# A planner's cost for ScalarE, and a state-space layer put in its written order

## The chip, the cores and the metric

The kernel runs on one core of a Trainium2 chip, in one launch. The metric is device time in microseconds; the time before is the median of three runs. Every execution timed here is of the whole network: eight layers, from the load of `x` to the store of the output.

## The reference

Four blocks of two layers each act on `x` of 8 sequences by 256 positions by 128 features. Every layer is wrapped as `x = x + layernorm(layer(layernorm(x)))`, where this layernorm has no weights. All data is float32. The layers are a gated delta rule, a local attention, a Plücker attention, a ternary feed-forward net, an attention, a mixture of experts, a two-way state-space layer (Mamba) and a quantized feed-forward net. The change touches the first six through one number of a planner, and the seventh, Mamba, in its code. What the seventh computes:

```python
def _mamba(x, W_in, conv_w, conv_b, W_xp, W_dt, dt_b, A_log, Dp, W_out):
    xp, z = split(x @ W_in.T)
    xc = silu(causal_conv4(xp) + conv_b)                 # E = 256 channels
    dt_lo, Bm, Cm = split(xc @ W_xp.T)                   # N = 64 states
    dt = softplus(dt_lo @ W_dt.T + dt_b)
    A = -exp(A_log)
    # for every position t:
    #   h = exp(dt * A) * h + (dt * xc)[:, :, None] * B[:, None, :]
    #   y = sum over n of h[:, :, n] * C[n]
    y = (y + xc * Dp) * silu(z)
    return y @ W_out.T

xn = layernorm(x) * ln1_w + ln1_b
x1 = _mamba(xn, m1)
x2 = flip(_mamba(flip(xn), m2))
out = layernorm(x1 + x2) * ln2_w + ln2_b + xn
```

As the wrapper normalizes `x` before the call, the layer's first layernorm is the second of two in a row on the same data. A second layernorm of a row with variance v has the variance v/(v+eps), so both together divide by sqrt(v*(1+eps) + eps*eps) if they are done as one.

## The kernel before

**The first six layers** are cut into small tasks (Python generators). A planner, the class `Turns`, runs them: it keeps a clock for each engine, adds the estimated time of each instruction that a task's step issues (`issued`), and always picks the live step that could begin first. The time that it gives an instruction of ScalarE (ACT) is `190 + 0.83 n` ns for n elements per partition, whatever the source, and 1283 ns more when the table of functions changes. The order that comes out is nailed down by `as_written`, which ties each instruction of the tensor engine (PE), VectorE (DVE), ACT and GpSimd (POOL) to the one before it on the same engine. The estimate decides more than the order: `Turns.evac` gives a copy out of PSUM to ACT or to DVE, whichever clock is behind, and `Turns.ps` fills gaps of PE with spare matmuls.

**Layer seven, `l3_attn`**, is not tied: its program order is a wish, and the framework's scheduler may issue ready instructions of an engine in another order. Its work is 8 units: four groups of two sequences (512 columns), each with two directions (m = 0 and 1). A unit's recurrence is done one state at a time, 64 states, so the loop has 8 x 64 = 512 steps `i`. In step `i` the program writes:

- `pre`: POOL makes the tile `dB` (one for two odd states, L2040);
- `inputs` of state i-1: PE writes `ps_h` in PSUM, by transposes of `sT` (even states, L2068) or by 64x64 matmuls (odd states, L2066);
- `start` of state i: a DMA brings `Cs`; ACT makes `sT` (even states, four instructions, L2050) and `dA` (two exponentials, L2053);
- `scan` of state i-1: DVE's scan (L2074) makes `h` from `dA` and `ps_h`; POOL multiplies it by `Cs` into `hc` (L2076); in every eighth state DVE does this product too;
- `add` of state i-4: PE adds `hc` to `ps_y` by transposes (L2086).

A unit also has a `prologue` (norm for m = 0, convolution, projections, SiLU, softplus: everything up to `dt`, `dtxT`, `B`, `cd`), and an `epilogue` (copy of `ps_y`, product with silu(z), output projection, and for m = 1 the norms and the residual). Both are generators: each `yield` hands over to the next step of the loop, so a `yield` between a producer and its consumer is a distance of one state in program order. The prologue of unit u+1 starts at state 6 of unit u; the epilogue of unit u-1 starts in unit u when its last state has been added. `norm_steps` is used by all layers: statistics on DVE (L227, L228), the power -1/2 on POOL (L230, L231), four `yield`s, a product on DVE (L234), one `yield`, and four ACT instructions (L237).

The buffers that set distances: `h`, `dA`, `sT` and `dB` have three each, `Cs` five, `hc` four. PSUM has three slots of two banks for `ps_h` and for every intermediate product `ps_a` of prologue and epilogue together (the function `pb`), and one slot of two banks for `ps_y`.

Of the kernel before, what the change touches and what calls it, by code (L numbers as in the profile page):

```python
# [17 lines left out]
P = 128  # L18
NB = 8
L = 256  # L20
# [152 lines left out]
class Ctx:  # L173
# [46 lines left out]
    def norm_steps(self, dst, src, n):  # L220

        nc = self.nc
        st = self.small.tile([P, n, 6], F32, name="ln_st")
        mv = self.small.tile([P, n, 2], F32, name="ln_mv")
        rs = self.small.tile([P, n], F32, name="ln_rs")
        for i in range(n):
            nc.vector.bn_stats(out=st[:, i, :], in_=src[:, i, :])  # L227
            nc.vector.bn_aggr(out=mv[:, i, :], in_=st[:, i, :])  # L228
        yield
        nc.gpsimd.tensor_scalar(rs, mv[:, :, 1], EPS, None, ALU.add)  # L230
        nc.gpsimd.tensor_tensor(rs, rs, self.mhalf.to_broadcast([P, n]), ALU.pow)  # L231
        for i in range(4):
            yield
        nc.vector.scalar_tensor_tensor(mv[:, :, 0], mv[:, :, 0], -1.0, rs, ALU.mult, ALU.mult)  # L234
        yield
        for i in range(n):
            nc.scalar.activation(dst[:, i, :], src[:, i, :], AF.Identity, bias=mv[:, i, 0:1], scale=rs[:, i:i + 1])  # L237
        yield
# [46 lines left out]
class Turns:  # L285
# [105 lines left out]
    def issued(self, ins):  # L391
# [6 lines left out]
        if "PE" in e:  # L398
            self.matmul(ins, aps)
            return  # L400
        elif "Pool" in e:
            t = 350.0 + (1.6 if n > 64 else 160.0 if "pow" in str(getattr(ins, "op", "")) else 2.0) * n
        elif "Act" in e:
            t, f = 190.0 + 0.83 * n, str(getattr(ins, "func", ""))
            table = next((x for x in ("Silu", "Gelu", "Sqrt") if x in f), "Exp" if "Exp" in f or "Tanh" in f else self.tables)
            if table != self.tables:
                self.tables, t = table, t + 1283.0
        else:
            t = (165.0 if op != "TensorScalarPtr" else 205.0) + 1.03 * n
# [1438 lines left out]
def l3_attn(k):  # L1848
# [17 lines left out]
    with ExitStack() as es:  # L1866
# [10 lines left out]
        for m, w in enumerate(k.l3a):  # L1877
# [8 lines left out]
            nc.vector.tensor_scalar(w["A"], w["A"], 1e-20, -1.0, ALU.max, ALU.mult)  # L1886
        xTs, CLs = [], []
# [21 lines left out]
        def prologue(u, o):  # L1909
            g, m = divmod(u, 2)  # L1910
            w = k.l3a[m]
            if m == 0:
                xs = xns[g] = s2.tile([P, 4, D], F32, name="xn")
                yield from k.norm_steps(xs, k.x[:, 4 * g:4 * g + 4, :], 4)
                yield from k.norm_steps(xs, xs, 4)
                nc.gpsimd.tensor_tensor(xs, xs, over(k.l3a_ln[:, 0, :], 4, 1), ALU.mult)
                nc.gpsimd.tensor_tensor(xs, xs, over(k.l3a_ln[:, 1, :], 4, 1), ALU.add)
                yield
            xT, CL = xTs[u % 2], CLs[u % 2]
            ps = pb()  # L1920
            for j in range(4):
# [3 lines left out]
                else:  # L1925
                    nc.tensor.matmul(ps[:, 0, d], xns[g][:, j ^ 1, :], k.flip, start=True, stop=True)
            yield
# [5 lines left out]
            for ec in range(2):  # L1933
                for b in range(2):
# [3 lines left out]
                    yield  # L1938
                    nc.scalar.activation(xc[:, ec, b * L:(b + 1) * L], ps[:, 0, 0:L], AF.Identity, bias=w["cols"][:, ec, 0:1])
                    yield  # L1940
                    yield
            for ec in range(2):
                ps = pb()
                nc.tensor.matmul(ps[:, 0, :], w["win"][:, 256 + ec * P:256 + (ec + 1) * P], xT[:, :, 3:3 + L], start=True, stop=True)
                yield
# [11 lines left out]
            yield  # L1957
            B = s2.tile([P, 4, N], F32, name="B")
# [10 lines left out]
            yield  # L1969
            nc.scalar.activation(dt, ps, AF.Softplus)  # L1970
# [6 lines left out]
            yield  # L1977
            dtxT = s2.tile([P, 4, 2, P], F32, name="dtxT")
            ps = pb()
            for j in range(4):  # L1980
                for ec in range(2):
                    n = 2 * j + ec
                    nc.tensor.transpose(ps[:, n // 4, n % 4 * P:(n % 4 + 1) * P], dtx[:, ec, j * P:(j + 1) * P], k.ident)
            yield
# [3 lines left out]
        def epilogue(u, o):  # L1988
# [4 lines left out]
            yield  # L1993
            py = pb()
# [3 lines left out]
            yield  # L1998
            t = s2.tile([P, 2, U], F32, name="t", tag="sp_u")
            for ec in range(2):  # L2000
                nc.vector.scalar_tensor_tensor(t[:, ec, :], o["xc"][:, ec, :], w["cols"][:, ec, 2:3], py[:, ec, :], ALU.mult, ALU.add)
            yield
            nc.gpsimd.tensor_tensor(t, o["sz"], t, ALU.mult)
# [6 lines left out]
            xs = s2.tile([P, 4, D], F32, name=f"x1{m}")  # L2010
            yield
# [8 lines left out]
            yield  # L2020
            xs = x1s[g]
            nc.vector.tensor_tensor(xs, ps[:, 0, :].rearrange("p (i d) -> p i d", d=D), xs, ALU.add)
            yield from k.norm_steps(xs, xs, 4)
# [5 lines left out]
            yield  # L2029
            yn = s2.tile([P, 4, D], F32, name="yn")  # L2030
            yield from k.norm_steps(yn, xs, 4)
# [38 lines left out]
        def scan(st, n):  # L2070
# [4 lines left out]
            st["hc"] = s1.tile([P, 2, 2, L], F32, name="hc", bufs=4)  # L2075
            (nc.vector if on_v else nc.gpsimd).tensor_tensor(st["hc"], h, over(by_seq(st["C"]), 2, 2), ALU.mult)  # L2076

        def add(o, st, n):

            if n == 0:  # L2080
                o["py"] = psumy.tile([P, 4, 2, P], F32, name="ps_y")
            for b in range(2):
                for j in range(2):
                    for ec in range(2):
                        first = n == 0 and j == ec == 0
                        nc.tensor.matmul(  # L2086
                            o["py"][:, 2 * b + j, ec, :], st["hc"][:, b, ec, j * P:(j + 1) * P], k.ident,
                            start=first, stop=n == N - 1, is_transpose=True, skip_group_check=True,
# [10 lines left out]
        for i in range(units * N + 4):  # L2099
# [15 lines left out]
            if i >= 4:  # L2115
                v, c = divmod(i - 4, N)
                add(made[v], sts.pop(i - 4), c)
# [57 lines left out]
def program(tc, I, out, layers):  # L2175
    nc = tc.nc
    with ExitStack() as es:
# [39 lines left out]
        for layer in (l3_attn, l3_ffn):  # L2217
            if layer in layers:
                layer(k)
# [20 lines left out]
```

## Time and profile before

| what | us |
|---|---|
| median of three runs | 4112.87 |
| the three runs | 4107.72 to 4126.58 |
| the profiled execution, its own time | 4108.04 |
| its span, first to last instruction | 4106.3 |
| start of the first scan of layer seven | 2671.2 |
| end of DVE's last product of layer seven | 4022.96 |
| busy in the whole span: PE, DVE, ACT, POOL | 3556.8, 3015.5, 2541.2, 2651.4 |

Times within the execution are counted from the start of the span. Busy times are unions of an engine's instructions; a wait is idle time of an engine, put down to what ended it. A busy PE is not PE at its peak, since matmuls are pipelined: the distance from start to start tells its rate.

### The profile page before, as it was taken

To read this page: it belongs to the slowest core of one execution; us is meant where nothing else is said; L and a number is where in the kernel's file an instruction comes from. 1 tells how busy PE (TensorE), PEld (TensorE's weight loads), DVE (VectorE), ACT (ScalarE), POOL (GpSimd) and SP (SyncE) were. 2 spreads that over 40 slices of the span, in tenths; PEclk is the share of its full clock that TensorE was granted. 3 is DMA by queue.
4 is the path that set the end of the run, shared out by engine and by line. 5 is a ranking of instruction groups with operands and counts; after the bars stand their busy time and mean duration, and the time that the engine had idled before them with its cause. 6 is when DMAs were issued, how large, how long until landed. Compare 5 with 4: busy or idle time off the path is not lost. (4 is left out here: it accounts for less than half of the span.)

```text
span 4106.3 us, 125005 instructions
## 1 busy us (share of the span) xinstructions
PE 3556.8 (87%) x55183; PEld 2808.9 (68%) x55183; DVE 3015.5 (73%) x4210; ACT 2541.2 (62%) x4481; POOL 2651.4 (65%) x1991
## 2 busy tenths in 40 slices
PE   6899898988898888899998977698988988898886
PEld 4777787777777656565565554387777876877774
DVE  7667768767666666654477677289979988998995
ACT  4445455544445545565454443399979988898893
POOL 5666857856665554522133344389989988998993
PEclk8999999999999999999999998799999999999997
DMA  2000000000001000000000000033323333333430
GB/s 58 3 3 2 3 3 2 3 3 8 3 23 34 1 1 12 20 6 21 1 1 1 6 1 1 26 105 112 110 81 116 111 100 93 111 112 91 115 114 26
DMA packets 98677, 168.89 MB, mean 41 GB/s; under 512 B 16699, under 2 KB 26582, under 8 KB 98006
## 3 DMA queue, kind: packets, MB, share of 16 engines
q1 hardware_dynamic: 98134, 160.89, 13.2%
q8 instruction: 433, 7.09, 0.7%
q14 instruction: 110, 0.90, 0.1%
HBM read 153.51 MB, written 2.10 MB: 38 GB/s over the span
## 5 line engine op out<-in xcount | busy, mean ns | idle before, releaser
L2076 POOL TENSOR_TENSOR hc<-h,Cs 128x1024 f32<-128x1024 f32 x448 | 1050.1, 2373 | 97.8 <-DVE h L2074 85.8
L2074 DVE TENSOR_TENSOR_SCAN h<-dA,ps_h 128x1024 f32<-128x1024 f32 x448 | 989.1, 2267 | 88.9 <-PE ps_h L2068 54.0
L2053 ACT ACTIVATE dA<-dt,A 128x512 f32<-128x512 f32 x1024 | 684.4, 715 | 125.1 <-DVE h L2074 92.2
L2086 PE MATMUL ps_y<-w_c_ident,hc 128*128 128x128 f32 x4096 | 560.9, 281 | 116.1 <-POOL hc L2076 84.1
L2086 PEld LDWEIGHTS ps_y<-w_c_ident,hc 128*128 128x128 f32 x4096 | 453.0, 143 | 171.4 <-POOL hc L2076 156.0
L2050 ACT ACTIVATE sT<-dtxT,B 128x256 f32<-128x256 f32 x1024 | 449.8, 495 | 5.7 <-PE ps_h L2068 5.7
L590 DVE SCALAR_TENSOR_TENSOR acc<-ps,w_l0a_conv,acc 128x254 f32<-128x254 f32 (+2 forms) x768 | 310.3, 472 | 46.9 <-ACT acc L584 46.7
L2066 PE MATMUL ps_h<-dB,dtxTt 64*64 64x64 f32 x16384 | 301.8, 223 | 19.3 <-DVE h L2074 10.1
L2066 PEld LDWEIGHTS ps_h<-dB,dtxTt 64*64 64x64 f32 x16384 | 266.2, 136 | 72.9 <-issue 46.4
L2068 PE MATMUL ps_h<-w_c_ident,sT 128*128 128x128 f32 x2048 | 277.3, 280 | 19.5 <-DVE h L2074 16.9
L2068 PEld LDWEIGHTS ps_h<-w_c_ident,sT 128*128 128x128 f32 x2048 | 240.2, 145 | 31.6 <-DVE h L2074 23.9
L742 POOL TENSOR_TENSOR Ps<-M,w_c_levels 128x512 f32<-128x512 f32 x192 | 241.3, 1274 | 7.2 <-DVE M L716 6.2
L230 POOL TENSOR_SCALAR ln_rs<-ln_mv 128x4 f32<-128x4 f32 (+1 forms) x84 | 22.0, 263 | 336.8 <-DVE ln_mv L228 307.0
L359 ACT COPY XY<-ps 128x1024 f32<-128x1024 f32 (+1 forms) x116 | 108.6, 947 | 152.8 <-PE ps L807 140.5
L800 PE MATMUL ps<-Z,XY 64*64 64x64 f32 x4608 | 169.5, 224 | 21.8 <-DVE Z L784 14.5
L807 PE MATMUL ps<-XY,Z 64*64 64x64 f32 x5120 | 168.8, 222 | 3.5 <-issue 3.5
L800 PEld LDWEIGHTS ps<-Z,XY 64*64 64x64 f32 x4608 | 142.1, 135 | 42.2 <-DVE Z L784 19.3
L1633 ACT ACTIVATE e<-ps,nm 128x256 f32<-128x256 f32 x256 | 99.9, 481 | 96.8 <-DVE nm L1630 69.5
L781 PE MATMUL ps<-XY,Ps 64*64 64x64 f32 x5120 | 115.9, 226 | 48.4 <-issue 11.7
L2074 DVE TENSOR_TENSOR_SCAN ps_h<-dA,ps_h 128x1024 f32<-128x1024 f32 x64 | 145.6, 2275 | 14.9 <-PE ps_h L2066 14.6
L784 DVE TENSOR_TENSOR Z<-ps,w_c_ident 128x512 f32<-128x512 f32 x160 | 107.8, 686 | 60.1 <-PE ps L781 58.6
L807 PEld LDWEIGHTS ps<-XY,Z 64*64 64x64 f32 x5120 | 148.6, 136 | 4.2 <-issue 4.2
(452 smaller groups left out, 8559.8 us busy)
## 6 DMA issues: line engine op xcount, KB each, us to landing
Cs<-cd SPq DMA_DIRECT2D x512, 256.0 KB, 3.3
dtxTt<-dtxT SPq DMA_DIRECT2D x32, 128.0 KB, 4.0
wk<-in_l0a_w SPq DMA_DIRECT2D x8, 256.0 KB, 6.8
w_h<-in_l1f_h SPq DMA_DIRECT2D x4, 512.0 KB, 6.0
w_l2a<-in_l2a_w SPq DMA_DIRECT2D x3, 512.0 KB, 3.8
w_l0a_wg<-in_l0a_wg SPq DMA_DIRECT2D x1, 1024.0 KB
w_qk<-in_l0f_wqkv SPq DMA_DIRECT2D x2, 512.0 KB, 5.3
cv<-in_l3a_m_conv SPq DMA_DIRECT2D x2, 512.0 KB, 4.9
```

Source lines behind the costliest of these rows:

```text
L590: nc.vector.scalar_tensor_tensor(acc[:, n, s:L], p4[:, n, 0:L - s], conv[:, h2, 4 * j + n, 3 - s:4 - s], acc[:, n, s:L], ALU.mult, ALU.add,)
L742: nc.gpsimd.tensor_tensor(t, M[:, :, 0:64], over(k.l0a_levels[:, n, :], 8, 1), ALU.mult)
L781: nc.tensor.matmul(ps[to, a, at(j)], Ps[own, h, :], XY[own, t, at(i)], start=True, stop=True)
L800: nc.tensor.matmul(ps[own, a, at(j)], XY[rows, t, at(i)], Z[rows, za, at(zj)], start=True, stop=True)
L807: nc.tensor.matmul(ps[to, a, at(4 + j)], Z[rows, za, at(zj)], XY[rows, t, at(i)], start=True, stop=True)
L2050: nc.scalar.mul(st["s"][:, j], o["dtxT"][:, j], o["B"][:, j, n:n + 1])
L2053: nc.scalar.activation(dA[:, :, ec, :], by_seq(o["dt"][:, ec, :]), AF.Exp, scale=w["A"][:, ec, n:n + 1])
L2066: nc.tensor.matmul(ps[q, b, ec, j * 64:(j + 1) * 64], o["dtxTt"][rows, j, ec, q], dB[rows, j, :], start=True, stop=True)
L2068: nc.tensor.transpose(ps[:, j // 2, ec, j % 2 * P:(j % 2 + 1) * P], st["s"][:, j, ec, :], k.ident)
L2074: nc.vector.tensor_tensor_scan(h.rearrange(flat), st["dA"].rearrange(flat), st["in"].rearrange(flat), 0.0, ALU.mult, ALU.add)
L2076: (nc.vector if on_v else nc.gpsimd).tensor_tensor(st["hc"], h, over(by_seq(st["C"]), 2, 2), ALU.mult)
L2086: nc.tensor.matmul(o["py"][:, 2 * b + j, ec, :], st["hc"][:, b, ec, j * P:(j + 1) * P], k.ident, start=first, stop=n == N - 1, is_transpos ...
```

## The change

1. The planner's estimate for an ACT instruction of the first six layers: `140 + 0.83 n` ns where an input lies in PSUM, `310 + 0.75 n` where all lie in SBUF.
2. `l3_attn` is put under `as_written` for PE, DVE, ACT and POOL.
3. `add` works on state i-5 in place of i-4; `hc` has five buffers.
4. More `yield`s in prologue and epilogue: two in place of one between most PE products and the copies that read them; in the norms three before and three after the product on DVE.
5. The two layernorms at the head of the layer are one, with the variance of both (`twice`).
6. `xc * D`: before, two DVE instructions with `D` as a scalar (L2001) in the epilogue. After, eight fp32 matmuls of `xc` by a diagonal tile `D` begin the sum in `ps_y`; DVE's single product takes `ps_a` and silu(z), and POOL's product `t` (L2003) goes.

```diff
-    def norm_steps(self, dst, src, n):
+    def norm_steps(self, dst, src, n, twice=False, steps=(4, 1)):
...
-        nc.gpsimd.tensor_scalar(rs, mv[:, :, 1], EPS, None, ALU.add)
+        if twice:
+            nc.gpsimd.tensor_scalar(rs, mv[:, :, 1], 1.0 + EPS, EPS * EPS, ALU.mult, ALU.add)
+        else:
+            nc.gpsimd.tensor_scalar(rs, mv[:, :, 1], EPS, None, ALU.add)
         nc.gpsimd.tensor_tensor(rs, rs, self.mhalf.to_broadcast([P, n]), ALU.pow)
-        for i in range(4):
+        for i in range(steps[0]):
             yield
         nc.vector.scalar_tensor_tensor(mv[:, :, 0], mv[:, :, 0], -1.0, rs, ALU.mult, ALU.mult)
-        yield
+        for i in range(steps[1]):
+            yield
...
-            t, f = 190.0 + 0.83 * n, str(getattr(ins, "func", ""))
+            near = any(a.bass_ap.space == PSUM for a in aps[len(ins.outs):])
+            t, f = 140.0 + 0.83 * n if near else 310.0 + 0.75 * n, str(getattr(ins, "func", ""))
...
+            w["D"] = s1.tile([P, 2, P], F32, name="D", bufs=2)
+            for ec in range(2):
+                nc.vector.tensor_scalar(w["D"][:, ec, :], k.ident, w["cols"][:, ec, 2:3], None, ALU.mult)
...
-                yield from k.norm_steps(xs, k.x[:, 4 * g:4 * g + 4, :], 4)
-                yield from k.norm_steps(xs, xs, 4)
+                yield from k.norm_steps(xs, k.x[:, 4 * g:4 * g + 4, :], 4, True, (3, 3))
...
             t = s2.tile([P, 2, U], F32, name="t", tag="sp_u")
-            for ec in range(2):
-                nc.vector.scalar_tensor_tensor(t[:, ec, :], o["xc"][:, ec, :], w["cols"][:, ec, 2:3], py[:, ec, :], ALU.mult, ALU.add)
-            yield
-            nc.gpsimd.tensor_tensor(t, o["sz"], t, ALU.mult)
+            nc.vector.tensor_tensor(t, py, o["sz"], ALU.mult)
+            yield
             yield
             yield
...
-            st["hc"] = s1.tile([P, 2, 2, L], F32, name="hc", bufs=4)
+            st["hc"] = s1.tile([P, 2, 2, L], F32, name="hc", bufs=5)
...
             if n == 0:
                 o["py"] = psumy.tile([P, 4, 2, P], F32, name="ps_y")
+                for j in range(4):
+                    for ec in range(2):
+                        nc.tensor.matmul(
+                            o["py"][:, j, ec, :], o["xc"][:, ec, j * P:(j + 1) * P], w["D"][:, ec, :],
+                            start=j % 2 == ec == 0, stop=False, skip_group_check=True,
+                        )
...
-            if i >= 4:
-                v, c = divmod(i - 4, N)
-                add(made[v], sts.pop(i - 4), c)
+            if i >= 5:
+                v, c = divmod(i - 5, N)
+                add(made[v], k.l3a[v % 2], sts.pop(i - 5), c)
...
-                layer(k)
+                with as_written(tc, COMPUTE if layer is l3_attn else ()):
+                    layer(k)
```

The further lines of the diff are single `yield`s: one more before the ACT copies of `xT`, the convolution, `sz`, `CL` and `B`, `dt`, `dtxT`, and `x1`, one more before the transposes of `yT` and one after them, one more before DVE's sum of `x1` and `x2`, two more before the transposes of `dtx`, three more before the transposes of `xn`, and one before the last norm.

## The prediction

> **What bounds the kernel now.** I read the page's head and slices first, then the busy times cut by the 8 units of layer seven, then who waited for whom on DVE in that loop, then the timeline of its worst stretch.
>
> ```profile
> span 4106.3 us, 125005 instructions
> PE 3556.8 (87%) x55183; PEld 2808.9 (68%) x55183; DVE 3015.5 (73%) x4210; ACT 2541.2 (62%) x4481; POOL 2651.4 (65%) x1991
> ```
>
> No engine is full over the span, but the shares mix two regimes. Up to about 2620 us the first six layers run, with PE busiest. The loop of layer seven, first scan 2671.2 to last product 4022.96, is 1351.8 us. I cut it where each unit's first scan starts (units 0, 1, 2, 6, 7; columns are the stretch, its length, then busy time of PE, PEld, DVE, ACT, POOL, the granted clock, the DMA share, GB/s):
>
> ```profile
> 2671.20:2832.60 161.40, 146.81 (x2888) 127.93 (x2891) 150.29 (x72) 151.37 (x283) 147.54 (x73) 0.97 0.36 108
> 2832.60:2995.90 163.30, 147.88 (x2924) 130.81 (x2920) 151.86 (x75) 149.08 (x275) 151.79 (x76) 0.99 0.37 110
> 2995.90:3182.00 186.10, 157.22 (x2936) 138.03 (x2934) 158.62 (x112) 156.03 (x291) 164.44 (x90) 0.94 0.32 97
> ...
> 3694.60:3870.10 175.50, 151.23 (x2940) 133.33 (x2936) 155.12 (x95) 152.33 (x283) 159.50 (x84) 0.98 0.37 103
> 3870.10:4022.90 152.80, 132.95 (x2833) 118.94 (x2821) 150.87 (x75) 129.29 (x241) 148.33 (x72) 0.99 0.36 109
> ```
>
> Unit 7, which prepares no other, takes 152.8 us with DVE busy 150.87: DVE is the floor (in the timeline eight states of a bare stretch take 18.7 us from scan to scan, 2.34 a state), and ACT and POOL stand within some per cent of it wherever a prologue runs. Unit 2 (unit 4 is its twin with 186.7) takes 33 us more than unit 7, of which only 8 are work of DVE. So the loop loses to DVE's idle time. DVE's waits within the loop:
>
> ```profile
> DVE h L2074 <- PE ps_h L2068: 54.0, 17, 35.7
> DVE ln_mv L234 <- POOL ln_rs L231: 30.4, 10, 3.7
> DVE h L2074 <- PE ps_h L2066: 15.9, 15, 3.2
> DVE ps_h L2074 <- PE ps_h L2066: 14.6, 6, 3.4
> DVE ln_st L227 <- POOL x L2028: 13.3, 3, 4.5
> DVE t L2001 <- PE ps_a L1997: 8.3, 7, 1.9
> DVE h L2074 <- POOL hc L2076: 8.2, 9, 1.8
> ```
>
> The 35.7 in the first line is the start of the layer; without it all waits come to 119 us, and 1229 busy plus 119 waiting make up the loop. Two rows, 30.4 and 13.3, are norm instructions at the head of DVE's queue, with ready scans behind them:
>
> ```profile
> 3031.49 0.17 DVE L234 SCALAR_TENSOR_TENSOR ln_mv<-ln_mv,ln_rs 128x4 f32<-128x4 f32 x1 [3.06 <-POOL ln_rs L231]
> ...
> 3038.30 0.29 DVE L227 BATCH_NORM_STATS2 ln_st<-x 128x6 f32<-128x128 f32 x1 [4.44 <-POOL x L2028]
> ```
>
> The same stretch of unit 2 shows norms of `xn`, which the program writes in unit 3: the scheduler pulled them forward, and put L234 right behind POOL's power.
>
> **The change part by part.**
>
> *Written order and the new distances in the norms.* After the change POOL's power stands at least three states ahead of L234. `h` has three buffers, so the scan just ahead of L234 cannot start before POOL has finished the product that stands just ahead of the power; the power (1.04 plus 0.23 us) then fits beneath that scan (2.2 us). For L227 <- x there are two states now. Both rows should go: -43.7 us. L2001's 8.3 has a further state of distance; I take -5.
>
> *One norm fewer.* In the timeline four pairs of L227/L228 take 1.05 us and L234 0.17: 1.25 us of DVE for each of the three groups normed within the loop: -3.7. ACT loses 1.65 and POOL 1.3 each; not counted, as DVE is the floor.
>
> *D by PE.* DVE: two of L2001 take 1.41 us (timeline); one product of 1024 from PSUM is 1.22 (row of L2076 on DVE). Seven epilogues in the loop: -1.3. POOL loses 2.37 each, which lies in its own idle time except where POOL is late; 0 here. PE gains 8 matmuls a unit. The rows, start to start:
>
> ```profile
> 3015.26 1.95 PE L2009 MATMUL ps_a<-w_l3a_m_wout,t 128*128 128x128 f32 x16
> 3018.78 1.04 PE L2068 MATMUL ps_h<-w_c_ident,sT 128*128 128x128 f32 x8
> ```
>
> The first are full fp32 matmuls, the second transposes, same size. The 16 follow each other at 0.11 us, as do the 8. The Trainium skill, "TensorE: Matmul & The Clock Gate", section "Terms", says that the transpose mode is 4 times faster for fp32. By that rule the new matmuls cost 0.44 us each, 3.5 us in one step, against a state's 2.34; `ps_h` of the next state would come 1 to 2 us late, 8 to 16 us over 8 units. By the row it is 0.9 us, and PE is busy only 133 of 152.8 us in unit 7. I take the row: 0. They also wait for ACT's copy of the previous `ps_y`, as L2086 does now (15.8 us in all on PE, not on DVE); behind them stands the next `inputs`, which has two scans of time.
>
> *Longer hold of PSUM.* A second `yield` keeps a `ps_a` slot one state (2.34 us) longer. With one slot held, `inputs` has two left and still runs beneath a scan. With two held (epilogue of m = 1 beside a convolution, units 2, 4, 6) it starts only when a scan ends, and its 1.04 to 1.16 us show. Bounds: from -20 us (in-order PE cures half of the 49 us of ps_h waits left) to +60 (nine long PE groups in each of seven units, 1 us each). I take +8, nearest to what unit 2 shows now (7 us of ps_h waits), for seven such overlaps in each of three units at a third of 1.1 us.
>
> *ACT in written order.* Its copies now stand at fixed places before the next `dA`. ACT leads by two states (three `dA`), so a copy that waits under about 4 us costs nothing. The load of tables stays: 14 of them with `dA` in the loop. Taken as 0; its failure is the third rival.
>
> *`add` one state later.* PE's waits for `hc` (row L2086, 82 us) are off DVE's path; 0, or slightly below. One more `hc` buffer goes with it. `Cs` and its queue on SP keep five buffers and their order.
>
> *Start of the layer.* Written order puts DVE's two `wk` (1.2 each), two `A` (0.26) and the new four `D` tiles (0.23 each, by L218's pitch) ahead of the first statistics, which now run at 2616 to 2618 beside the last layer's. From 2627.9: 3.8 us to 2631.7, statistics 1.05, POOL 1.35, L234 0.2, ACT 1.7, POOL's two products 2.7 gives 2638.8, where PE now begins at 2633.9: +5.0, with the saved norm already in it. Then ACT must do `dtxT`, `sT`, the table load (1.28) and `dA` in that order, where `dA` and its load came early: +1.3.
>
> *End of the layer.* The last epilogue lies bare: POOL's 2.34 and 0.2 of DVE and a hop go: -2.7.
>
> *The planner's numbers.*
>
> ```profile
> L359 ACT COPY XY<-ps 128x1024 f32<-128x1024 f32 x98 | 98.8, 1014 | 145.5 <-PE ps L807 133.6 <-issue 5.4 <-POOL ln_rs L231 3.7
> ...
> L237 ACT ACTIVATE xn<-x,ln_mv,ln_rs 128x128 f32<-128x128 f32 x80 | 32.9, 489 | 11.4 <-DVE ln_mv L234 11.4
> ```
>
> For the first the old formula says 1040 and the new 990; measured 1014. For the second 296 and 406; measured 32.9/80 = 411. The Trainium skill, "ScalarE: Activation LUTs", section "Rules for kernel authors", budgets about 0.3 us plus 0.83 ns an element whatever the source: 1150 and 406. By that rule the new constant for PSUM is a step the wrong way; by the row both errors are small. The instructions stay the same either way; only their order and some copies' engine move. ACT is half busy there and PE's chains bind. I take 0, bounds -25 and +30 (about 1% of 2620 us).
>
> **Sum.** Loop: -43.7 - 5 - 3.7 - 1.3 + 8 = -45.7. Edges: +5.0 + 1.3 - 2.7 = +3.6. Together -42.1 on the profiled execution's 4108.0 (its span is 4106.3): 4065.9. That execution was 4.8 below the median, so I forecast 4071.
>
> **The rivals.** The likeliest, as summed, has a chance of 0.66; its own range is 4040 to 4095.
>
> *PSUM becomes the bound* (0.12). For: three slots, already 49 us of ps_h waits, longer holds. Against: ps_h is not late in the bare unit 7. At the upper bound +60 in place of +8 the sum is +10: 4123, no difference.
>
> *ACT's queue starves the scans: slower* (0.11). Twelve ACT instructions a unit wait for a PE group, 84 in seven units, and `dA` is behind each. It decides once PE is more than two states (4.7 us) late, as it may be at the projection that fills `B`, 4.2 us of PE (rows L1953 and L1956, 33.9 us for 8). At 1.1 us each it costs 92: +50 net, 4163.
>
> *The first six layers decide* (0.11). Reordering there is worth more than its even chance: at -25, 4046; at +30, 4101. A sub-case is that the order hardly moves.
>
> **How the numbers follow.** About 0.5% (20.6 us) is what a measurement of this kernel can tell from no change. Faster by more, under 4092: most of the first case, most of the last: 0.71. Within: 0.17. Slower: 0.12. The range 4025 to 4115 leaves out the ACT case and the worst of PSUM's above, a loop with every wait gone (-119) below.
>
> **What would show it.** Right: units 2 and 4 fall from 186 to about 167, unit 6 from 175.5 to 166, units 1, 3, 5 stay at 163 to 166 as the norms move there; DVE's rows L234 <- POOL and L227 <- POOL vanish in the loop; the first scan comes later after the sixth layer's end. Wrong: a steady eighth of a unit above 18.7 us, rows of DVE waiting for `dA` or `ps_h` grown past 60 us, or a start of layer seven that moves by over 25 us.

## The result: slower by 0.44%, and the profile after

The changed kernel takes 4135.93 us (median of 14 runs, 4122.69 to 4148.04), the kernel before beside it 4116.81 (14 runs, 4105.26 to 4129.47). The ratio is 1.0044, with a 95% interval of 1.0028 to 1.0059: a small loss, where the forecast was 4071 and a gain. Its profiled execution took 4136.71. The head of its page:

```profile
span 4134.9 us, 125432 instructions
PE 3591.7 (87%) x55322; PEld 2823.3 (68%) x55322; DVE 3005.2 (73%) x4150; ACT 2518.4 (61%) x4475; POOL 2624.1 (63%) x1975
```

The shares of busy time are those of before within two points, so nothing is seen here. The span has to be cut where the prediction cut it. The layers before Mamba end with POOL's last addition to `x`, which the timelines of before and of after have as follows:

```profile
2622.24 1.26 POOL L1822 TENSOR_TENSOR x<-x,y 128x512 f32<-128x512 f32 x1 [0.98 <-ACT y L237]
```

```profile
2680.16 1.26 POOL L1828 TENSOR_TENSOR x<-x,y 128x512 f32<-128x512 f32 x1 [1.96 <-ACT y L242]
```

From there on, in us:

| stretch | before | after | difference | forecast |
|---|---|---|---|---|
| start to the end of the sixth layer | 2623.5 | 2681.4 | +57.9 | 0 (bounds -25, +30) |
| from there to the first scan | 47.7 | 52.5 | +4.8 | +6.3 |
| first scan to DVE's last product | 1351.8 | 1315.3 | -36.5 | -45.7 |
| from there to the end of the span | 83.3 | 85.6 | +2.3 | -2.7 |
| span | 4106.3 | 4134.9 | +28.6 | -42.1 |

So the loop gave most of what was forecast, and six layers whose work is the same as before, but for 11 spare matmuls and the engine of some copies, took it back one and a half times over. The loop by units, as in the prediction (units 0, 1, 2, 6, 7; the stretch, its length, busy PE, PEld, DVE, ACT, POOL, granted clock, DMA share, GB/s):

```profile
2733.90:2892.90 159.00, 147.00 (x2937) 128.78 (x2934) 150.59 (x73) 147.70 (x279) 147.50 (x74) 0.98 0.36 108
2892.90:3055.70 162.80, 148.66 (x2931) 131.09 (x2930) 153.79 (x84) 147.41 (x279) 153.02 (x79) 1.00 0.36 110
3055.70:3227.60 171.90, 151.58 (x2942) 132.26 (x2941) 158.48 (x94) 149.47 (x283) 156.85 (x83) 1.00 0.35 105
...
3725.10:3897.10 172.00, 151.61 (x2942) 132.29 (x2941) 158.54 (x94) 149.54 (x283) 156.88 (x83) 1.00 0.39 105
3897.10:4049.30 152.20, 132.75 (x2792) 118.97 (x2790) 150.80 (x74) 128.04 (x246) 147.22 (x72) 1.00 0.37 109
```

Units 2 and 4 fell from 186 to 172 us, unit 6 from 175.5 to 172; the bare unit 7 still stands on DVE's 150.8. DVE's waits in the loop:

```profile
DVE h L2093 <- ACT dA L2072: 44.6, 7, 41.4
DVE h L2093 <- PE ps_h L2085: 21.5, 18, 3.1
DVE ps_h L2093 <- PE ps_h L2085: 17.3, 8, 4.3
DVE h L2093 <- PE ps_h L2087: 11.5, 11, 1.3
DVE h L2093 <- POOL hc L2095: 10.6, 12, 1.8
DVE ps_h L2093 <- ACT dA L2072: 4.2, 3, 1.4
DVE h L2093 <- ACT sT L2069: 3.4, 3, 1.8
```

41.4 of the first row is the start of the layer. Without it DVE waits 71.7 us, against 119.3 before. The rows for `ln_mv` and `ln_st` (43.7 us) and for L2001 (8.3) are gone, as forecast. The three `ps_h` rows make 50.3 in place of 48.8 by the same sum of before's page (84.5 less the start's 35.7). What is new is small: `sT`, and some more for `dA` and `hc`.

### The profile page after: what moved, and what is told of

It is laid out like the page before. It is cut to its first block, busy times and chain, and to the rows that moved or that the text cites. A ratio compares the mean times of both kernels' runs of the same rounds, so it can differ in the third digit from the quotient of the medians.

```text
span 4134.9 us, 125432 instructions
## 1 busy us (share of the span) xinstructions
PE 3591.7 (87%) x55322; PEld 2823.3 (68%) x55322; DVE 3005.2 (73%) x4150; ACT 2518.4 (61%) x4475; POOL 2624.1 (63%) x1975
## 4 chain that ended last, share of the span: by engine, by line
PE 42%; POOL 21%; DVE 17%; issue 13%; ACT 6%; DMA 0%; POOLq 0%; ACTq 0%; DVEq 0%; SPq 0%
POOL hc L2095 12%; PE ps L1524 3%; POOL dB L2059 2%; DVE acc L596 2%; PE ps L584 2%; PE ps L1380 2%; DVE h L2093 2%; PE ps L787 1%; PE ps L806 1%; PE ps L813 1%; PE ps L1683 1%; PE ps L860 1%; PE ps L880 1%; PE ps L895 1%; PE ps L920 1%
## 5 line engine op out<-in xcount | busy, mean ns | idle before, releaser
L2093 DVE TENSOR_TENSOR_SCAN h<-dA,ps_h 128x1024 f32<-128x1024 f32 x448 | 993.4, 2269 | 93.5 <-ACT dA L2072 44.6
L2072 ACT ACTIVATE dA<-dt,A 128x512 f32<-128x512 f32 x1024 | 673.9, 712 | 141.8 <-DVE h L2093 139.6
L2110 PE MATMUL ps_y<-w_c_ident,hc 128*128 128x128 f32 x4096 | 550.7, 278 | 68.0 <-POOL hc L2095 64.7
L2069 ACT ACTIVATE sT<-dtxT,B 128x256 f32<-128x256 f32 x1024 | 434.0, 496 | 0.0
L596 DVE SCALAR_TENSOR_TENSOR acc<-ps,w_l0a_conv,acc 128x253 f32<-128x253 f32 (+2 forms) x768 | 309.1, 472 | 79.0 <-ACT acc L590 78.7
L2085 PEld LDWEIGHTS ps_h<-dB,dtxTt 64*64 64x64 f32 x16384 | 264.8, 135 | 71.7 <-issue 48.8
L2087 PE MATMUL ps_h<-w_c_ident,sT 128*128 128x128 f32 x2048 | 277.7, 276 | 20.6 <-DVE h L2093 10.4
L234 POOL TENSOR_SCALAR ln_rs<-ln_mv 128x4 f32<-128x4 f32 (+1 forms) x76 | 19.3, 253 | 401.9 <-DVE ln_mv L229 366.6
L2087 PEld LDWEIGHTS ps_h<-w_c_ident,sT 128*128 128x128 f32 x2048 | 229.4, 141 | 46.6 <-ACT sT L2069 22.1
L2093 DVE TENSOR_TENSOR_SCAN ps_h<-dA,ps_h 128x1024 f32<-128x1024 f32 x64 | 145.5, 2274 | 21.5 <-PE ps_h L2085 17.3
```

The lines of the kernel that those rows point to most:

```text
L596: nc.vector.scalar_tensor_tensor(acc[:, n, s:L], p4[:, n, 0:L - s], conv[:, h2, 4 * j + n, 3 - s:4 - s], acc[:, n, s:L], ALU.mult, ALU.add,)
L2069: nc.scalar.mul(st["s"][:, j], o["dtxT"][:, j], o["B"][:, j, n:n + 1])
L2072: nc.scalar.activation(dA[:, :, ec, :], by_seq(o["dt"][:, ec, :]), AF.Exp, scale=w["A"][:, ec, n:n + 1])
L2085: nc.tensor.matmul(ps[q, b, ec, j * 64:(j + 1) * 64], o["dtxTt"][rows, j, ec, q], dB[rows, j, :], start=True, stop=True)
L2087: nc.tensor.transpose(ps[:, j // 2, ec, j % 2 * P:(j % 2 + 1) * P], st["s"][:, j, ec, :], k.ident)
L2093: nc.vector.tensor_tensor_scan(h.rearrange(flat), st["dA"].rearrange(flat), st["in"].rearrange(flat), 0.0, ALU.mult, ALU.add)
```

## The experiments

Each kernel is the changed one with the edit shown, unless it says that it is the one before. Theories differ on where the 58 us come from: the estimate's new order of the first six layers, something else in the change, or the clock that TensorE is granted. All results in one place (us; end of the sixth layer, first scan, and loop are of the profiled execution; the time is a median where there are several runs; "product" is the start of the last feed-forward product of layer two, used further below):

| kernel | product | sixth layer ends | first scan | loop | time (runs) |
|---|---|---|---|---|---|
| before | 1819 | 2623.5 | 2671.2 | 1351.8 | 4116.81 (14) |
| after | 1953 | 2681.4 | 2733.9 | 1315.3 | 4135.93 (14) |
| e1_old_estimate | 1830 | 2636.9 | 2689.4 | 1315.3 | 4073.59 (6) |
| e2_estimate_alone | 1958 | 2686.9 | 2732.5 | 1352.7 | 4168.22 (4) |
| e3_near_alone | 1921 | 2706.7 | 2759.3 | 1315.3 | 4159.84 (1) |
| e4_far_alone | 1871 | 2663.8 | 2716.3 | 1315.3 | 4117.31 (1) |
| e5_flat_180 | 1904 | 2657.0 | 2709.5 | 1315.4 | 4110.24 (1) |
| e5_flat_188 | 1806 | 2640.1 | 2692.5 | 1315.2 | 4094.14 (1) |
| e5_flat_192 | 1905 | 2651.3 | 2705.3 | 1315.4 | 4106.88 (1) |
| e5_flat_200 | 1999 | 2737.1 | 2789.4 | 1315.7 | 4191.13 (1) |
| f1_new_fill500 | 1973 | 2696.0 | 2748.4 | 1315.3 | 4150.75 (4) |
| f2_old_fill500 | 1838 | 2648.7 | 2702.3 | 1315.3 | 4103.93 (12) |
| m1_written_order_alone | 1833 | 2628.7 | 2684.4 | 1392.1 | 4165.32 (1) |
| m2_no_written_order | 1818 | 2624.2 | 2663.1 | 1335.2 | 4080.82 (1) |
| g1_new_less2 | 1910 | 2685.5 | 2739.5 | 1315.6 | 4143.71 (1) |
| g2_new_more2 | 1835 | 2630.2 | 2682.7 | 1315.5 | 4085.32 (1) |
| g3_new_near90 | 1970 | 2683.2 | 2735.7 | 1315.6 | 4137.10 (1) |
| k1_four_back | 1821 | 2617.2 | 2669.4 | 1339.1 | 4094.01 (1) |
| h1_new_last_group_ahead | 1898 | 2681.4 | 2734.0 | 1315.9 | 4126.20 (5) |
| h2_old_last_group_back | 2146 | 2668.6 | 2720.8 | 1315.5 | 4121.23 (9) |

Two things can be read from it before any single run. The loop of layer seven repeats to 0.7 us in the fifteen kernels that have all its edits, wherever it starts. And the old order of the first six (before, e1, m1, m2, k1) ended them between 2617.2 and 2636.9: one order scatters by 20 us, so a single profile tells orders apart only beyond that.

**The change in two: the estimate and the rest.** e1 gives the changed kernel its old estimate back; e2 gives the kernel before the new one and nothing else.

```diff
-            t, f = 140.0 + 0.83 * n if near else 310.0 + 0.75 * n, str(getattr(ins, "func", ""))
+            t, f = 190.0 + 0.83 * n, str(getattr(ins, "func", ""))
```

> The kernel after with one edit undone: the planner's estimate for ScalarE is again 190 + 0.83 n. Theory A (the new estimate's order of the first six layers costs what was lost): the first scan of layer seven comes at 2671 + 5 = 2676 us, as the first six layers are planned as before, the loop of layer seven stays at 1315 us, and the whole is 4117 - 36 + 5 + 2 = 4088 us, faster than before by 0.7%. Theory B (the edits of layer seven slow the first six, by memory held or by what stands at the border): the first scan stays at 2734 us and the time at 4136 us.

> The kernel before with one edit: the planner's new estimate for ScalarE, layer seven as it was. Theory A: the first scan at 2671 + 58 = 2729 us, the loop of layer seven at 1352 us as before, the whole at 4117 + 58 = 4175 us, slower by 1.4%. Theory B: 4117 us, no change.

Beside 4109.88 for the kernel before, e1 took 4073.59, ratio 0.9918 (0.9887 to 0.9948), and e2 4168.22, ratio 1.0139 (1.0098 to 1.0179). So the layer's part is worth -36.3 us and the estimate +58.3; together +22.0, where the whole change measured +19.1. The two parts add up, and the loss is the estimate's. The first six layers of before, after and e1 in one row each:

```profile
0.00:2623.50 2623.50, 2296.96 (x31679) 1714.64 (x31679) 1744.29 (x3355) 1297.65 (x2191) 1379.42 (x1329) 0.95 0.03 9
```

```profile
0.00:2681.40 2681.40, 2337.32 (x31690) 1735.97 (x31690) 1726.60 (x3326) 1306.42 (x2201) 1377.83 (x1327) 0.94 0.03 9
```

```profile
0.00:2636.90 2636.90, 2316.76 (x31679) 1729.43 (x31679) 1743.48 (x3346) 1296.71 (x2191) 1372.48 (x1327) 0.94 0.03 9
```

The work is the same to within 20 us on DVE, ACT and POOL. PE is busy 40 us longer for 11 more records, at a slightly lower clock, and 18 us longer idle (2681.4 - 2337.3 against 2623.5 - 2297.0). Neither copies that moved between engines nor more work explain 58 us. e1 is also the best of the kernels with several runs: it beats both before and after.

**Which half of the estimate?** e3 has the new number for PSUM and the old for SBUF, e4 the reverse.

```diff
+e3            t, f = 140.0 + 0.83 * n if near else 190.0 + 0.83 * n, ...
+e4            t, f = 190.0 + 0.83 * n if near else 310.0 + 0.75 * n, ...
```

> The kernel after with half of the new estimate: 140 + 0.83 n for a source in PSUM, the old 190 + 0.83 n for one in SBUF. If the lower figure for PSUM is what hurts (theory A1: ScalarE looks free too early and is given more copies), the first scan comes at about 2730 us. If the higher figure for SBUF hurts (A2), it comes at about 2676 us. If any other number gives just another draw of the order (A3), it lies anywhere within some tens of us of both, and this run and the next do not add up to the whole 58 us.

> The kernel after with the other half: 310 + 0.75 n for a source in SBUF, the old 190 + 0.83 n for one in PSUM. A1: first scan at about 2676 us. A2: about 2730 us. A3: anywhere between 2650 and 2740 us, with no sum that fits the run before this one.

Against e1's end of 2636.9, e3 ends 70 us later, e4 27, and both halves together 45. They don't add up, and neither number is "the wrong one".

**Is there a trend in the number?** The old form with 180, 188, 192 and 200 in place of 190:

```diff
+            t, f = 180.0 + 0.83 * n, ...   # and 188.0, 192.0, 200.0
```

> The kernel after with a flat 180 + 0.83 n, 10 ns under the old one. A3: as with 188, unrelated to its result: no trend with the constant. A4: a small part, a fifth, of what 140 did (83 us), so about 2690 us.

> The kernel after with a flat estimate of 188 + 0.83 n for ScalarE, 2 ns (about half a per cent of a typical instruction) under the old one. Theory A3 (a list schedule is a draw: any change of an estimate that flips a choice gives another order of the first six layers, and the order before was a lucky one): the first scan of layer seven moves by 10 to 60 us from the 2676 to 2689 us of the old estimate, mostly later. Theory A4 (accuracy or direction counts: only a change of tens of ns matters): first scan within 15 us of 2680.

> The kernel after with a flat 192 + 0.83 n, 2 ns over the old one. A3: another order, first scan moved by 10 to 60 us, mostly later. A4: within 15 us of 2680.

> The kernel after with a flat 200 + 0.83 n, 10 ns over the old one. A3: no trend, mostly later than the old one by 10 to 60 us. A4: 2665 to 2690 us.

Ten ns more ended the six layers 100 us later than e1, ten ns less 20 us, two ns more 14. 188 and 192 lie within the scatter of one order, or near it; 200 doesn't. The end does not follow the number in one direction: each value is another order, and the orders tried lie in a range of 120 us. By themselves the five values would also fit a valley around 190; g2, further below, with two other numbers, speaks against that. The timeline of the last addition with 200:

```profile
2735.87 1.26 POOL L1828 TENSOR_TENSOR x<-x,y 128x512 f32<-128x512 f32 x1 [1.96 <-ACT y L242]
```

**Is it the clock?** By the rows above, PE's granted clock was 0.94 in place of 0.95. The planner's `IDLE` sets from which gap on PE is filled with spare matmuls; 500 in place of 1500 ns more than doubles them (790 records in place of 330 with the new estimate, 782 in place of 319 with the old).

```diff
-    HOP, SWITCH, IDLE, NEAR = 150.0, 150.0, 1500.0, 100.0
+    HOP, SWITCH, IDLE, NEAR = 150.0, 150.0, 500.0, 100.0
```

> The kernel after with one number changed: the gap that the planner leaves to PE before it fills with spare matmuls (IDLE) is 500 ns in place of 1500. The order on the other engines is the same as in the kernel after; PE gets 790 spare matmuls in place of 330. It asks what the slower order is slow by. Theory C (the order leaves PE gaps, the gaps lower PE's granted clock, and the low clock makes up most of the loss: in the kernel after the first six layers lose 173 us of clock against 132 in the profile before): the lost clock falls to about 140 us and the first scan comes 20 to 35 us earlier, at about 2705 us. Theory D (the idle time itself is the loss, chains of PE, DVE and ACT that the order sets out badly; the clock only follows): the clock rises, but the first scan stays within 10 us of 2734, or comes later by the time of the spare matmuls.

> The old estimate 190 + 0.83 n with all edits of layer seven, and IDLE 500 in place of 1500 (782 spare matmuls in place of 319). Theory C: the 132 to 160 us of lost clock fall to about 120 and the time falls from 4074 to about 4055 us. Theory D: 4074 us or up to 15 us more.

The first six layers of f1 and of f2:

```profile
0.00:2696.00 2696.00, 2403.44 (x32150) 1753.30 (x32150) 1716.61 (x3326) 1306.12 (x2201) 1376.32 (x1327) 0.95 0.03 8
```

```profile
0.00:2648.70 2648.70, 2365.08 (x32142) 1731.10 (x32142) 1740.34 (x3346) 1297.38 (x2192) 1377.34 (x1327) 0.97 0.03 9
```

The clock came back: with the clock's loss counted as time times (1 - granted clock) up to the end of the sixth layer, the six layers lost 171 us in after, 132 in f1, 132 in before; 158 in e1, 91 in f2. The time did not: f1 took 4150.75 (ratio to before 1.0108, 1.0078 to 1.0138), about 15 us more than after; f2 took 4103.93 (0.9992, 0.998 to 1.0004), some 30 more than e1. DVE's order in f1 is that of after. So spare matmuls do not buy the loss back. This alone does not clear the clock, since the spare matmuls take PE's time themselves (busy 2403.4 us in f1, 2337.3 in after), and after lost 39 us more of clock than before, about as much as its PE was busy longer.

The other traces allow an estimate of the clock's part. In the five profiles of the old order the lost clock (120 us in k1, 132 in before, 135 in m2, 139 in m1, 158 in e1) and the end of the sixth layer (2617.2 to 2636.9) rise together, at 0.53 us of time for one of lost clock. Over the executions of one kernel the rate is 0.65 to 0.92, for each of the eight sets of five or more. If the lost clock is what lengthened them, then after's 39 us more make, as an estimate, 20 to 36 of the 58 us. The rest needs another cause: g1, further below, lost 162 us, 5 more than e1, and ended its six layers 49 us later.

**Is it something coarse in the new estimate?** g1 and g2 shift both numbers by 2 ns; g3 changes the grain at which the planner takes two starts for equal.

```diff
+g1            t, f = 138.0 + 0.83 * n if near else 308.0 + 0.75 * n, ...
+g2            t, f = 142.0 + 0.83 * n if near else 312.0 + 0.75 * n, ...
+g3    HOP, SWITCH, IDLE, NEAR = 150.0, 150.0, 1500.0, 90.0
```

> The kernel after with 2 ns less in both levels of the estimate (138 and 308). Theory A3 (a draw): the first scan lies 15 us or more from the 2734 us of the kernel after, to either side, within 2675 to 2790. Theory A5 (the two levels are worse as such): within 12 us of 2734, the scatter of one order from run to run.

> The kernel after with 2 ns more in both levels (142 and 312). A3: 15 us or more from 2734 to either side, and not the mirror of the run before. A5: within 12 us of 2734.

> The kernel after with the new estimate as it is, and the width within which the planner counts two starts as equal (NEAR) at 90 in place of 100 ns: no engine's estimate is touched. A3: another draw, 15 us or more from 2734. A5: within 12 us of 2734.

g2 is 51 us earlier than after with 2 ns more, as good as the old estimate: two numbers in place of one are not worse as such. g1 and g3 came within 5 us of after, though their orders differ from it widely. For these two the bet on a draw, 15 us or more away, was lost, and theory A5 had the distance right: the free scatter that the other draws suggest is not seen in them.

**What late orders have in common.** In every trace the product that ends a feed-forward group of layer two (eight of them, two for each group of sequences) can be found. DVE's rows of that tile, for before, after, and g2 (behind the colon durations in ns, which agree; then the times of the first and the last instance, which are what matters):

```profile
L1216 DVE TENSOR_TENSOR y<-ps,y x8: 691/692/693, 1374.2 to 1819.2; 128x512 f32<-128x512 f32 x8
```

```profile
L1222 DVE TENSOR_TENSOR y<-ps,y x8: 682/691/692, 1413.0 to 1952.9; 128x512 f32<-128x512 f32 x8
```

```profile
L1222 DVE TENSOR_TENSOR y<-ps,y x8: 691/692/692, 1394.2 to 1835.2; 128x512 f32<-128x512 f32 x8
```

Over the first 18 kernels of the table, the last instance and the end of the six layers go together (correlation 0.91): all eight at or below 1838 end by 2649, all ten from 1871 on end after 2651. The 18 are only 11 different orders: six of the early eight have the old one, and after, e2 and f1 share the new one. Without f1 and f2, and with one mean for each order, the correlation is 0.86, and that of the lost clock with the end is 0.93. In late orders, more steps of layer three are taken ahead of layer two's last group: before its product DVE has done 53 to 57 instructions of layer three in the early eight, and 77 to 130 in the late ten. Two kernels test whether that is the cause: in the planner's choice they move that group alone, forward under the new estimate (h1) and back under the old one (h2).

```diff
-                key = (max(ready, free) // self.NEAR, order)
+                key = ((max(ready, free) - (1000.0 if task[3][:2] == ("l0f", 1) and task[3][3:4] in ((3,), (6,), (7,)) else 0.0)) // self.NEAR, order)
```

h2 is e1 with -500.0 in the place of 1000.0.

> The changed kernel, new estimate; in the planner's choice of the next step the tasks of layer two's second half that belong to the fourth group of sequences (its last group) count as able to begin 1 us earlier than they are. Up to the first four of that layer's eight feed-forward groups DVE's order is that of the changed kernel; the last of the eight now stands at DVE's instruction 2199 in place of 2264 (2217 under the old estimate). If the late last group costs the time: its product comes at or before 1850 us (1952.9 in the changed kernel), the six layers end at 2620 to 2650, the first scan stands at 2672 to 2705, the loop keeps 1315, and the time is 4070 to 4105. If the late group only accompanies late orders: the six layers end at 2665 to 2700 as in the changed kernel, and the time is 4120 to 4155. In between (2650 to 2665) neither is shown.

> The changed kernel with the old estimate; the same tasks count as able to begin 0.5 us later than they are. DVE's order is that of the old estimate up to the first four groups, and the last of the eight stands at DVE's instruction 2539 in place of 2217. If the late last group costs the time: its product comes after 1950 us, the six layers end at 2670 or later (2636.9 with the old estimate unbiased, 2617 to 2637 in five executions of that order), and the time is 4110 or more. If it only accompanies late orders: the six layers end at 2615 to 2650 though the group is late, and the time is 4055 to 4100.

```profile
L1222 DVE TENSOR_TENSOR y<-ps,y x8: 684/692/692, 1412.8 to 1898.1; 128x512 f32<-128x512 f32 x8
```

```profile
L1222 DVE TENSOR_TENSOR y<-ps,y x8: 690/692/692, 1373.0 to 2146.3; 128x512 f32<-128x512 f32 x8
```

The first line is h1's: the product came 55 us earlier than in after (not the 100 that I had expected), and the six layers ended at 2681.4, not a microsecond earlier. Its time was 4126.20, ratio to before 1.0054 (1.0035 to 1.0072). h2's product came 317 us later than in e1, and the end only 32 later, at 2668.6, just short of the 2670 that I had named; its time was 4121.23, ratio to before 1.0035 (1.0015 to 1.0055), where e1 had 0.9918. By these medians h2 is 53 us behind e1, whose profiled execution was its slowest. So a group left behind can cost something, a tenth to a sixth of its own delay here, but nothing shows that it holds the changed kernel back: brought forward, it brought nothing. That test went less than half the way, though, since 1898 is still far from the 1819 to 1838 of the early orders. As far as is seen, the late group accompanies late orders, as the low clock does. What makes one of them late on the chip stays open.

**Layer seven: written order or distances?** m1 is the kernel before with `as_written` on layer seven and nothing else; m2 is e1 without it.

```diff
+m1 (before)     with as_written(tc, COMPUTE if layer is l3_attn else ()):
+m1                  layer(k)
-m2              with as_written(tc, COMPUTE if layer is l3_attn else ()):
+m2              with as_written(tc, ()):
```

> The kernel before with one edit: layer seven tied to its written order (no other edit in it: norms with four and one steps, both norms, additions four back, D on DVE). If the order alone brings the gain, the loop of layer seven takes about 1315 to 1325 us. If the added distances are needed for it, the copies on ACT stand one state behind their PE products and hold dA up: the loop takes 1352 us or more. I expect something between, 1335 us: the norms' waits (44 us) go with the order, since four states stand between the power and its reader, and about 10 to 20 us of waits for ps_h and dA come.

> The kernel after with the old estimate and layer seven not tied to its written order (all other edits in place). If the order is what removes the norms' waits from DVE, those rows (L238 waiting for POOL, L228 waiting for POOL) come back and the loop takes 1335 to 1350 us. If the distances alone are enough, it takes 1315 us.

The loop is 1351.8 before, 1392.1 with the order alone, 1335.2 with the other edits alone, 1315.3 with both. My expectation for m1 was missed by 57 us and by its sign: nailing the order down without the distances costs 40 us. m1's waits of DVE and then of ACT in the loop show why:

```profile
DVE h L2074 <- ACT dA L2053: 57.1, 16, 41.5
DVE h L2074 <- PE ps_h L2066: 38.6, 10, 6.9
DVE h L2074 <- PE ps_h L2068: 27.5, 21, 5.8
DVE h L2074 <- ACT sT L2050: 27.4, 5, 7.6
...
DVE ln_st L227 <- POOL x L2028: 15.2, 3, 5.1
```

```profile
ACT x L2012 <- PE ps_a L2009: 37.8, 7, 6.2
ACT xz L1939 <- PE ps_a L1937: 13.7, 14, 2.0
```

ACT stands before a copy whose matmuls have not come (6.2 us at worst), and `sT` and `dA`, which a free scheduler would have issued, stand behind it; scans then wait for both (41.5 of the first row is the start of the layer). That is the prediction's third rival. It takes place in m1 and is gone in after, where ACT waits for PE nowhere in the loop. Of the edits between the two, the added `yield`s are those that stand between a product and its copy; no run has them alone. In m2 a norm's row is back:

```profile
DVE h L2093 <- PE ps_h L2085: 50.8, 23, 5.8
DVE h L2093 <- PE ps_h L2087: 48.8, 17, 30.9
DVE ln_mv L238 <- POOL ln_rs L235: 18.0, 6, 3.2
DVE h L2093 <- ACT dA L2072: 9.4, 9, 1.7
DVE ps_h L2093 <- PE ps_h L2085: 5.7, 8, 1.4
```

More distance in the program does not bind a scheduler that pulls L238 forward again. The waits for `ps_h` are longer as well: 74.4 us in m2 without the start's 30.9, and 50.3 in after. So the order needs the other edits, and without the order they give less than half of the gain.

**The addition, five states back or four.** k1 is e1 with `add` on i-4 and four `hc`, as in the kernel before.

```diff
-            st["hc"] = s1.tile([P, 2, 2, L], F32, name="hc", bufs=5)
+            st["hc"] = s1.tile([P, 2, 2, L], F32, name="hc", bufs=4)
-                add(made[v], k.l3a[v % 2], sts.pop(i - 5), c)
+                add(made[v], k.l3a[v % 2], sts.pop(i - 4), c)
```

> The kernel after with the old estimate, the additions four states back as before and four buffers of hc in place of five. If the fifth state matters, PE stands before its additions waiting for POOL's hc while the next ps_h is due, and the loop of layer seven rises from 1315 us by 10 us or more. I expect little, since PE's waits for hc were not on DVE's path: 1315 to 1322 us.

The loop is 1339.1, 24 us longer, where the prediction held this edit for 0 and the expectation of this run for 7 at most. PE's wait for `hc`, in k1 and then in after:

```profile
PE ps_y L2110 <- POOL hc L2095: 106.7, 121, 3.7
```

```profile
PE ps_y L2110 <- POOL hc L2095: 63.5, 111, 1.2
```

In the written order PE cannot pass the addition that waits, so the next `ps_h` waits with it, and DVE's scans for `ps_h` (in k1; after's rows, 11.5 and 21.5, stand in the section on the result):

```profile
DVE h L2093 <- PE ps_h L2087: 34.0, 24, 4.1
DVE h L2093 <- PE ps_h L2085: 27.5, 21, 2.6
```

## Why the prediction was wrong

**The step that failed is "The planner's numbers".** It says "I take 0, bounds -25 and +30 (about 1% of 2620 us)", because "The instructions stay the same either way; only their order and some copies' engine move. ACT is half busy there". Measured: +57.9 in the profile, +58.3 from e2's medians. The premise was right and the conclusion wrong: the same work in another order took 58 us more, 40 of them with PE busy and 18 with PE idle. A likely reason, argued and not tested, is that an order that a planner writes out and `as_written` nails down has no slack of the kind that a half-busy engine suggests, since every instruction waits for the one written before it. By the estimate above a lower granted clock goes with 20 to 36 of the 58 us, and the prediction did not weigh the clock. What in the new order costs the rest stays open. The bound was guessed, not taken from anything in the profile. The draws give it: the orders tried ended the six layers at 2617 to 2737. That both constants lay nearer to the measured ACT durations than the old one decided nothing: 142 was good, 140 and 138 were not. The Trainium skill's budget in "ScalarE: Activation LUTs", section "Rules for kernel authors", was no measure for it either: it is given for an activation with its bias as a pointer operand, which the copy L359 is not, and says nothing of the source (1150 by the budget, 1014 measured). The rival "the first six layers decide" named the place and had too small a size. Of the signs of being wrong one came: the first scan moved by 62.7 us, and the limit named was 25. For the rest of the change the sum was off by 6: -36.3 (e1 against before) for -42.1.

**The norms' waits:** right, -43.7, and L2001's row went entirely (-8.3 for -5). In sum DVE's waits fell by 47.6 us for a forecast of 40.7.

**DVE's own work** was mis-sized: forecast -3.7 and -1.3, measured +8.8 (1229.4 to 1238.2 busy in the loop). The -1.3 for `D` is right (L2001 9.8 us, the new product 8.5). Three norms fewer were counted, but two of before's lay ahead of its loop: L234's ten instances in it became nine. And the product of the norm got dearer by standing where it was put. Its rows in before and after:

```profile
L234 DVE SCALAR_TENSOR_TENSOR ln_mv<-ln_mv,ln_rs 128x4 f32<-128x4 f32 x10 | 3.8, 377 | 30.4 <-POOL ln_rs L231 30.4
```

```profile
L238 DVE SCALAR_TENSOR_TENSOR ln_mv<-ln_mv,ln_rs 128x4 f32<-128x4 f32 x9 | 8.9, 985 | 0.0
```

It waits for nothing any more, but runs for 985 ns instead of 377: +5.1 in all. The last section shows what it runs beside. Another +4.3 stands in the row of the 448 scans into `h` (989.1 to 993.4) and was not followed.

**`ps_h`:** forecast +8, measured +1.5. The units 2, 4 and 6 still came out at 172, not 167 or 166: in unit 2 DVE is busy 158.5 us, as before (158.6), and idle 13.4. The units 1, 3 and 5 took 162.7 to 162.8, just below the 163 to 166 forecast. The rival "PSUM becomes the bound" is not seen.

**D by PE:** both weighings were wrong. L2009's sixteen records are eight matmuls, since a full fp32 matmul leaves two records and a transpose one. After's timeline for the eight new matmuls:

```profile
2900.28 2.05 PE L2103 MATMUL ps_y<-D,xz 128*128 128x128 f32 x16 [1.26 <-ACT yT L2008]
```

That is 2.05 us, where I read 0.9 from the row and estimated 3.5 by what the Trainium skill says in "TensorE: Matmul & The Clock Gate", section "Terms": transposes 4 times faster. Beside the 1.04 us of eight transposes of the same size (L2068) it is 2 times here. DVE has no row of waiting for it.

**The addition** was held for nothing and is worth 24 us in this order (k1). The sum came out near e1 although it saw neither the 40 us that the written order alone costs nor the 24 that this distance gives; so its nearness is in part luck.

**Start of the layer:** +4.8 for +6.3, right in kind: PE begins 15.5 us after the sixth layer's end in place of 10.4, +5.1 for the +5.0 forecast. The further +1.3 for ACT did not show.

**End of the layer:** +2.3 for -2.7. POOL's product is gone, and from ACT's copy `yT` to its copy of the output projection the timeline has 6.91 us in place of 9.89. But `yT` comes later behind DVE's last product, as PE's last two additions start later and take longer; before, then after:

```profile
4022.89 1.97 PE L2086 MATMUL ps_y<-w_c_ident,hc 128*128 128x128 f32 x16 [1.22 <-POOL hc L2076]
4024.90 1.01 ACT L1992 COPY yT<-ps_y 128x1024 f32<-128x1024 f32 x1 [8.37 <-PE ps_y L2086]
```

```profile
4050.18 3.36 PE L2110 MATMUL ps_y<-w_c_ident,hc 128*128 128x128 f32 x16 [1.22 <-POOL hc L2095]
4053.58 1.01 ACT L2008 COPY yT<-ps_y 128x1024 f32<-128x1024 f32 x1 [10.78 <-PE ps_y L2110]
```

DVE's last product ended at 4022.96 and at 4049.23, so the copy starts 1.9 and 4.4 us after it: +2.4. Of these, 1.0 is the later start: POOL's last `hc`, for which PE waits, ends 0.1 us before DVE's last product in before and 0.9 after it in after. The other 1.4 is the longer duration: the clock granted in the stretch was 1.00 in before and 0.57 in after. The statistics in written order add 1.2: 0.5 in the first norm, whose pairs follow each other at 0.4 us where the free scheduler interleaved them at 0.26, and 0.8 in the second, where statistics of layer eight stand between them. The other 1.6 lie in layer eight and were not followed.

## What to carry to other kernels

A number that feeds a list scheduler can redraw the whole order. Its price is then the spread of draws, here 120 us of 2620 for changes of 2 to 120 ns, and its accuracy did not decide it; measure it apart from every other edit, and keep a good draw even when a "better" number is at hand. A written order and the distances that it needs are one edit: the order alone cost 40 us, the other edits of the layer without it gained 17, all together gained 37, and a single state of distance at PE was worth 24 of it. And before two orders are compared, look at the granted clock of each: here part of the difference went with it.

## What the hardware showed that was not expected

**A tiny DVE product lasts as long as POOL's running product.** From after's timeline:

```profile
3145.09 4.70 POOL L2095 TENSOR_TENSOR hc<-h,Cs 128x1024 f32<-128x1024 f32 x2
...
3148.05 1.77 DVE L238 SCALAR_TENSOR_TENSOR ln_mv<-ln_mv,ln_rs 128x4 f32<-128x4 f32 x1
```

Four elements per partition take 1.77 us and end at 3149.82, when POOL's second product ends (3149.79). All nine L238 of the loop end within 0.03 us of the end of POOL's running `hc`, and so do e1's nine; with POOL idle, as at the end of the layer, L238 takes 0.16. Before has both cases in its loop: right behind POOL's power, with POOL idle, the same instruction takes 0.17 us (eight times), and beside POOL's addition `x<-x,yn` 1.22 (twice):

```profile
3050.99 1.27 POOL L2033 TENSOR_TENSOR x<-x,yn 128x512 f32<-128x512 f32 x1
3051.05 1.22 DVE L234 SCALAR_TENSOR_TENSOR ln_mv<-ln_mv,ln_rs 128x4 f32<-128x4 f32 x1 [3.72 <-POOL ln_rs L231]
```

That the two share something is read from these times; no run took POOL's product away.

**Clock won by spare matmuls was not less time.** In the profiles f2 lost 67 us less clock than e1 (91 for 158) and ended its six layers 12 us later; by the medians it was 30 us slower. The spare matmuls that win the clock occupy PE themselves, busy 2365.1 us against 2316.8.
